# Local attention layers: one slot for both key tiles of half a batch's heads, with the previous slot's weighting behind it; the first sublayer's steps in two parts

## The chip, the cores and the metric

The kernel runs on one core of a Trainium2 chip. Its time is the time of one execution on the device, in microseconds (us); it was run three times. A profile comes from one further execution, whose time is given beside its span (first instruction to last). The engines are named PE (TensorE, matrix products and transposes; PEld is its loading of stationary operands), DVE (VectorE), ACT (ScalarE), POOL (GpSimd) and SP (SyncE, which issues DMAs). Each takes its instructions in the order in which they were issued to it. PE writes to PSUM, which is handed out in banks of 128 partitions x 512 f32.

## The reference: what is computed

The whole program is a chain of sublayers on x, 16 batches of 256 tokens with 128 channels. Two kinds of sublayer bear on the change: the first one of the chain, and the local attention layers, which are run as two pairs (after the first sublayer, and again after a performer sublayer), so four in all.

```python
def _L0_attn_a_ref(x, ...):                     # the first sublayer
    h = _layernorm(x, ln_g, ln_b)
    Q, K, V = h @ Wq.T, h @ Wk.T, h @ Wv.T
    y0 = K @ W0 + (K @ A_init) @ B_init
    gradient = K * (y0 - V)
    grad_shift = cumsum of gradient over the tokens before this one
    correction = Q * lr * grad_shift
    out = y0 - correction * pos_scale
    out = (out * sigmoid(x @ Wg.T)) @ Wo.T * ls_g
    return x + out

def _layer(x, ...):                             # one local layer
    h = shift_token(x)                          # half the channels come from the token before
    q, k, v = split(h @ wqkv, 3)                # 8 heads of 64 each
    q, k = l2norm(q) * qs, l2norm(k) * ksc
    q, k = rotary_xpos(q, k)                    # cos/sin tables over the position
    o = local_attention(q, k, v)                # blocks of 64 queries see their own and the previous block:
    #   mask = (i < j) | (i > j + 64); attn = softmax(where(mask, -max, 8 q k^T)); o = attn v
    x = x + o @ wo
    h = layernorm(shift_token(x)) * lg + lb
    a, g = split(h @ w1 + b1, 2)
    return x + (a * gelu(g)) @ w2 + b2
```

`_L0_attn_a_ref` normalises x with eps 1e-5; in the kernel a norm is made twice over for it, once more for the gate's input. All data are f32; only the mask's product runs in bf16.

## The kernel before

**Helpers.** `mm` (L504) and `tr` (L508) are PE's matmul and transpose; a matmul written out stands at L3465. `act` (L528) is an ACT instruction, `tt` (L531) and `stt` (L543) are DVE's, `gt` (L534) POOL's. All of a helper's instructions carry its line, so they are told apart by their tiles' names. `bank(tag)` (L510) hands out the next PSUM bank of a tag; the banks of a tag go round in order, and a bank is handed out again once everything that reads its last contents is done. `share` (L514) sets how many of the eight banks each tag has in a stage. Inside `manual_schedule` the order in which the program issues its instructions is the order on every engine.

**Tiling.** x and its companions lie with the channels on the partitions: 4096 tokens in 8 chunks of 512 (`NCH`, `CH`), or 32 tiles of 128 (`NTILE`). A batch of 256 tokens is two tiles.

**The first sublayer** (`l0_attn_a`, L1860 to L1947) is a pipeline of steps over the chunks, driven by `slots` (L1820): in slot k step i works on chunk k-i, and within a slot the steps run from the last to the first, and then the steps in `last`. The steps: `enter` (transposes of x), `centre` (`centre_step`, L1759: a product with a centring matrix, a copy by ACT, and a square `nsq` by POOL), `spread` (`spread_step`, L1774: a product with the mean matrix, then Ln and Exp by ACT, twice each), `scale` (two DVE products, and between them ACT's Identity, which adds the bias to `hb`), `gradient` (products for `k` and the error, ACT's copy of `k`, DVE's product and running sum, POOL's scaling by position), `correct` (products for the query, y and the gate; two DVE steps, ACT's Sigmoid, POOL's product with the gate), `out` (a product, DVE, POOL). `last` holds three steps of the next layer's norm, for its first five chunks (`lead`, L1834). ACT's Sigmoid and the Ln/Exp pair need different tables, so the table is loaded anew twice in a slot (`logs`, L1659).

**A local layer** (`local_layer`, L3340) is `local_attend` (L3347 to L3536) and then `local_ffn`, which the change leaves alone. The attention works tile by tile of 128 tokens:

- `project(n)` (L3372): the queries and keys of tile n, two products of 512 columns into two `w` banks; ACT squares both (`sq`), DVE multiplies both by the cosine and the sine table (`t1`, `t2`, four instructions).
- `rotate(n)` (L3390): DVE sums the squares to `ss` (16 values a token) and bounds them; POOL adds the rotated halves into `t1`.
- `unit(n)` (L3400): ACT's Ln and Exp turn `ss` into one over the norm, POOL scales `t1`.
- `turn(n)` (L3408): queries, then keys: four transposes into a `w` bank, which ACT copies to `qkt`; then the values, one product into a `w` bank, which ACT copies to `v`.
- `score(b, hg, t)` (L3423): batch b, half hg of the heads (four), key tile t. Two `s` banks. For t = 0 the four products have 192 columns (128 queries of the tile and 64 of the next), and DVE masks them by a minimum into `pt`, then ACT takes the exponent of both at once (768 columns). For t = 1 the products have 128 columns, and the mask is first put into each bank by a bf16 product of 256 columns; ACT takes the exponent straight from the bank, 256 columns a time. The products of two heads run on the two halves of the array's rows (64 x 128).
- `weigh(b, hg, t)` (L3452): the sums of the weights (a product with ones, bank `pd`) and the weighted values (bank `po`, two halves of 32 of the 64 channels), each as four products that take 32 of the array's columns (128 x 32). After t = 1 ACT takes Ln and Exp(-) of `pd`, into `rd`.
- `divide(b, hg)` (L3478): DVE multiplies `po` by `rd` into `ot`.
- `out(c)` (L3488): chunk c's output product from four slices of `ot`, added to z by DVE.
- `chunk_steps` (L3501): the steps of the norm of x for a chunk (`norm_x_step`, L1811; skipped for the chunks that the stage before has already led), the shift by one token (`shift`, L692, three POOL instructions), and the norm of the result for the feed-forward part (centre, spread, scale with ACT's Identity).

The loop (L3516 to L3536) runs over half-slots k, one for each (b, hg, t), so 64 in all and two for each token tile. In a half-slot the order is: `divide` (of half-slot k-4), `unit`, `score(k)`, `weigh(k-2)`, `project`, `rotate`, `turn`, `out`, `chunk_steps`. A tile is projected ten half-slots ahead of the scores that need it, turned five ahead. The banks: three of `w` (projections, transposes, values, outputs, norms), two of `s`, three of `o`.

Order of the bank requests of `w` in a tile's two half-slots: project twice, queries, keys, values.

Of the kernel before, what the change touches and what calls it, by code (L numbers as in the profile page):

```python
# [13 lines left out]
AF = mybir.ActivationFunctionType  # L14
ALU = mybir.AluOpType
# [1634 lines left out]
class Fast(Net):  # L1650
# [169 lines left out]
    def slots(self, n, *steps, last=(), every=1):  # L1820


        both = (*steps, *last)
        with self.tc.manual_schedule():
            self.logs()
            for k in range((n - 1) * every + len(both)):
                for i in (*reversed(range(len(steps))), *reversed(range(len(steps), len(both)))):
                    c, rest = divmod(k - i, every)
                    if rest == 0 and 0 <= c < n:
                        both[i](c)  # L1830
# [29 lines left out]
    def l0_attn_a(self, w):  # L1860
        nc = self.nc
        with self.second(), ExitStack() as st:
# [26 lines left out]
            sq, rs, cums, ys = {}, {}, {}, {}  # L1889
# [8 lines left out]
            def scale(c):  # L1898
# [3 lines left out]
                self.act(h, h, AF.Identity, bias=w["ln_b"])  # L1902
                self.tt(h0, h0, r1, ALU.mult)

            def gradient(c):
# [8 lines left out]
                self.act(k, pk, AF.Copy)  # L1914
                grad = p.tile([P, CH], F32, tag="grad", name="grad")
# [6 lines left out]

            def correct(c):
                wy, we, lr = made
                h0, h = self.ha[:, self.chunk(c)], self.hb[:, self.chunk(c)]
                pq, py, pg = self.bank(), self.bank(), self.bank()
                self.mm(pq, w["Wq"], h)
                self.mm(py, wy, h)
                self.mm(pg, w["Wg"], h0)
# [4 lines left out]
                g = p.tile([P, CH], F32, tag="g", name="g")  # L1934
                self.act(g, pg, AF.Sigmoid)
# [11 lines left out]
            self.slots(NCH, *first, centre, spread, scale, gradient, correct, out, last=self.lead(p, tables=True))  # L1947
# [1399 lines left out]
    def local_attend(self, w, z, hs, last):  # L3347
# [3 lines left out]

        nc = self.nc
        with ExitStack() as st:
# [16 lines left out]
            made, rot, qkt, val, weights, sums, outs, steps = {}, {}, {}, {}, {}, {}, {}, {}  # L3370
# [37 lines left out]
            def turn(n):  # L3408
                b, t = divmod(n, 2)
                if t == 0:  # L3410
                    qkt[b] = p.tile([P, 2, 4, T], F32, tag="qkt", name="qkt", bufs=2)
                t1, _ = rot.pop(n)
                for i in range(2):
                    pt = self.bank("w")
                    for g in range(4):
                        self.tr(pt[:, g * P : g * P + P], t1[:, i, 2 * g : 2 * g + 2])
                    self.act(qkt[b][:, i, :, t * P : t * P + P], pt.rearrange("p (g t) -> p g t", g=4), AF.Copy)
                pv = self.bank("w")
                self.mm(pv, hs[:, n * P : n * P + P], w["qkv"][:, 1024:])
                val[n] = p.tile([P, 512], F32, tag="v", name="v", bufs=6)  # L3420
                self.act(val[n], pv, AF.Copy)

            def score(b, hg, t):  # L3423
                wide = 192 - 64 * t
                qt, kt = qkt[b][:, 0], qkt[b][:, 1]
                ps = [self.bank("s"), self.bank("s")]
                pt = p.tile([P, 2, 384], F32, tag="pt", name="pt", bufs=4)
                if t:
                    for a in range(2):
                        self.mm(ps[a][:, :T], identb, self.twice(masked), stop=False)  # L3430
                for i in range(2):
                    g = 2 * hg + i
                    for a in range(2):
                        rows = slice(64 * a, 64 * a + 64)
                        self.mm(
                            ps[a][:, i * wide : i * wide + wide], kt[rows, g, t * P : t * P + P],
                            qt[rows, g, t * P : t * P + wide], start=t == 0, stop=t == 0 or i == 1,
                        )
                if t:
                    for a in range(2):  # L3440
                        self.act(pt[:, a, :T], ps[a][:, :T], AF.Exp)
                else:
                    for a in range(2):
                        self.tt(
                            pt[:, a].rearrange("p (i t) -> p i t", i=2), ps[a][:, :384].rearrange("p (i t) -> p i t", i=2),
                            self.twice(w["see"]), ALU.min,
                        )
                    flat = pt.rearrange("p a t -> p (a t)")
                    self.act(flat, flat, AF.Exp)
                weights[b, hg, t] = pt  # L3450

            def weigh(b, hg, t):  # L3452


                wide = 192 - 64 * t
                if t == 0:
                    sums[b, hg] = self.bank("o"), self.bank("o")
                pt = weights.pop((b, hg, t))
                pd, po = sums[b, hg]
                for half in range(-1, 2):  # L3460
                    for r in range(4):
                        i, a = divmod(r, 2)
                        d = (4 * hg + r) * 64 + 32 * half
                        at = max(half, 0) * T + t * P
# [330 lines left out]
```

## Time and profile before

| what | us |
|---|---|
| three runs | 4425.52, 4427.38, 4429.76 (median 4427.38) |
| the profiled execution | 4426.24 |
| its span, first instruction to last | 4424.4 |
| first sublayer, about 14 to 120 | 106 |
| four local attentions, 120-434, 503-799, 1182-1492, 1561-1857 | 314, 296, 310, 296 |
| PE busy in these four | 292, 281, 290, 281 |
| the two feed-forward parts behind the first and the third, 434-503, 1492-1561 | 69, 69 |

The profile is of one execution. Its busy times count, for each engine, the time in which an instruction of it was under way; PE's ends are modelled, so a matmul's start says more than its end. The granted clock is the share of full speed that PE was given; its mean over the span was 0.951. In tables by window the columns are: start and end, length, busy time of PE, PEld, DVE, ACT and POOL with the number of instructions in brackets, granted PE clock, DMA share, GB/s. In a timeline: start, busy time, engine, line, operation, out<-in, shapes, number of like instructions in a row, and in square brackets the idle time before it with what ended it.

In the second local attention (503 to 799) the largest waits were: DVE's multiplies for ACT's squares, 46.9 us in 32 cases; POOL's scaling for ACT's `ss`, 44.2 in 19; ACT's exponents for DVE's minima, 36.9 in 32. PE's own idle time before its groups is a few us in each: before the projections 2.8, before the scores 4.2, before the transposes 4.9.

### The profile page before, as it was taken

The numbers are of one execution on the slowest core, as the hardware profiler recorded it, in microseconds if no ns is written. First come the engines' busy times: TensorE is split into PE (matmuls) and PEld (weight loads), VectorE is DVE, ScalarE is ACT, GpSimd is POOL, SyncE is SP. The second block draws the span as 40 slices with busy tenths as digits, with TensorE's granted clock in tenths as the row PEclk, the third lists the DMA queues.
The fourth block names the chain that finished last, engine by engine and source line by source line (L and its number), as shares of the span: only waits on it lengthen the run. The fifth ranks groups of instructions, "written<-read, shape, count | busy, mean of one in ns | idle before, by whom it ended". The sixth has DMA issues, their size and how long they took to land. (4 is left out here: it accounts for less than half of the span.)

```text
span 4424.4 us, 70817 instructions
## 1 busy us (share of the span) xinstructions
PE 3989.1 (90%) x27720; PEld 2183.8 (49%) x27720; DVE 2620.2 (59%) x4477; ACT 2368.0 (54%) x4505; POOL 2129.9 (48%) x1790
## 2 busy tenths in 40 slices
PE   7899999999899999994989969897999999899978
PEld 3455455466355445553865548653333334355333
DVE  4765576364376376455336633464888788486474
ACT  6665466444766456553337633345565554675442
POOL 4653355232465165315433424465988788521251
PEclk8999999999999999997999979998999999999989
DMA  1800000000000000001630026200000000000000
GB/s 58 331 1 1 10 1 2 19 1 1 19 2 1 1 4 1 1 1 59 204 100 10 15 81 190 70 16 18 1 1 1 2 2 1 15 2 18 6 0 20
DMA packets 70390, 142.31 MB, mean 32 GB/s; under 512 B 11006, under 2 KB 39300, under 8 KB 69920
## 3 DMA queue, kind: packets, MB, share of 16 engines
q1 hardware_dynamic: 57120, 114.46, 7.9%
q0 software_dynamic: 9568, 18.51, 1.2%
q8 instruction: 222, 3.64, 0.3%
q10 hardware_dynamic: 3360, 4.72, 0.3%
q14 instruction: 120, 0.98, 0.1%
HBM read 84.22 MB, written 55.25 MB: 32 GB/s over the span
## 5 line engine op out<-in xcount | busy, mean ns | idle before, releaser
L528 ACT ACTIVATE pt<-ps 128x512 f32<-128x512 f32 (+1 forms) x896 | 423.1, 537 | 410.2 <-PE ps L504 408.8
L504 PE MATMUL ps<-hb,w 128*128 128x512 f32 (+1 forms) x960 | 467.8, 621 | 5.7 <-issue 3.3
L531 DVE TENSOR_TENSOR t<-ps,tab 128x512 f32<-128x512 f32 x512 | 319.6, 684 | 195.5 <-ACT sq L528 190.8
L504 PE MATMUL ps<-w,hb 128*128 128x512 f32 (+2 forms) x896 | 414.9, 576 | 13.8 <-DVE t L531 11.5
L534 POOL TENSOR_TENSOR t<-t,ss 128x1024 f32<-128x1024 f32 x128 | 243.5, 1902 | 309.1 <-ACT ss L528 199.9
L534 POOL TENSOR_TENSOR t<-t,t 128x512 f32<-128x512 f32 x256 | 320.3, 1273 | 13.2 <-PE ps L504 10.1
L504 PEld LDWEIGHTS ps<-hb,w 128*128 128x128 f32 (+1 forms) x960 | 181.9, 194 | 270.3 <-issue 242.2
L504 PE MATMUL ps<-nsq,ct 128*128 128x512 f32 x368 | 212.3, 662 | 70.4 <-POOL nsq L534 51.5
L534 POOL TENSOR_TENSOR nsq<-ha 128x512 f32<-128x512 f32 x112 | 122.5, 1094 | 315.3 <-ACT ha L528 298.7
L531 DVE TENSOR_TENSOR u<-u,ps 128x512 f32<-128x512 f32 x220 | 129.3, 591 | 216.4 <-PE ps L504 144.6
L528 ACT ACTIVATE pt<-pt 128x768 f32<-128x768 f32 (+1 forms) x160 | 169.6, 1060 | 155.4 <-DVE pt L531 155.4
L2185 POOL DMA_INDIRECT back<-y,x x156 | 152.7, 979 | 197.8 <-ACT y L528 171.9
L504 PE MATMUL ps<-qkt 64*128 64x192 f32 (+1 forms) x2048 | 216.9, 327 | 11.8 <-ACT pt L528 11.8
L504 PE MATMUL ps<-u,w 128*128 128x512 f32 (+1 forms) x448 | 218.2, 611 | 8.4 <-POOL u L534 8.4
L504 PE MATMUL ps<-ot,w 128*128 128x512 f32 x448 | 212.2, 607 | 14.8 <-POOL ot L534 6.6
L504 PE MATMUL ps<-xt,w 128*128 128x256 f32 x936 | 219.9, 385 | 4.1 <-DMA w<-in_moe_x 3.1
L504 PEld LDWEIGHTS ps<-qkt 64*128 64x128 f32 x2048 | 153.6, 189 | 134.6 <-ACT qkt L528 51.5
L531 DVE TENSOR_TENSOR pt<-ps,w 128x384 f32<-128x384 f32 (+1 forms) x320 | 171.3, 576 | 77.3 <-PE ps L504 73.9
L504 PEld LDWEIGHTS ps<-w,hb 128*128 128x128 f32 x896 | 147.1, 192 | 139.6 <-issue 110.6
L3692 POOL DMA_INDIRECT rows<-out,idx x128 | 126.3, 987 | 171.4 <-ACT out L528 121.7
L528 ACT ACTIVATE u<-ps,w 128x512 f32<-128x512 f32 x160 | 107.1, 685 | 186.4 <-PE ps L504 183.7
L531 DVE TENSOR_TENSOR pt<-pt,w 128x1024 f32<-128x1024 f32 (+1 forms) x96 | 181.1, 1887 | 42.6 <-ACT pt L528 42.6
(362 smaller groups left out, 9087.5 us busy)
## 6 DMA issues: line engine op xcount, KB each, us to landing
w<-in_moe_x SPq DMA_DIRECT2D x78, 533.0 KB
rows<-t SPq DMA_DIRECT2D x64, 520.0 KB
x<-rows SPq DMA_DIRECT2D x78, 130.0 KB
w<-in_local_f SPq DMA_DIRECT2D x8, 659.5 KB
y<-back SPq DMA_DIRECT2D x16, 256.0 KB
y<-back ACTq DMA_DIRECT2D x16, 256.0 KB
w<-in_local_f SPq DMA_DIRECT2D x4, 658.5 KB
back<-y,x POOLq DMA_INDIRECT x156
```

What stands on the lines that cost most here:

```text
L504: self.nc.tensor.matmul(out, lhsT, rhs, start=start, stop=stop)
L528: self.nc.scalar.activation(out, in_, func, **kw)
L531: self.nc.vector.tensor_tensor(out, a, b, op)
L534: self.nc.gpsimd.tensor_tensor(out, a, b, op)
L2185: nc.gpsimd.indirect_dma_start(views[2 * i + t], bass.IndirectOffsetOnAxis(ap=x[:, t, C : C + 1].bitcast(I32), axis=0), y[:, t], None, bou ...
L3692: nc.gpsimd.indirect_dma_start(views[(c * 2 + k) * 4 + t], bass.IndirectOffsetOnAxis(ap=idx[:, k, t : t + 1], axis=0), out[:, k, t], None,)
```

## The change

**In the first sublayer** a step may be a tuple of two parts. In a slot `slots` first runs part 0 of every step, from the last step to the first, then part 1 of every step that has one in the same order, then the steps in `last`. `scale` keeps its two DVE products as part 0, and the Identity becomes part 1 (`shift`). `gradient` is split behind ACT's copy of `k`: `keys` (products and copy) and the rest. `correct` is split behind the gate: `queries` (the gate's product now first, then query and y, and the Sigmoid) and the rest. No instruction is added or removed.

**In local attention** a slot m is a half of a batch's heads with both key tiles, so 32 slots, one for each token tile. `score(m)` takes four `s` banks: the mask is put into a 128-column piece of each by four bf16 products, then the eight products run one after the other, those of key tile 0 and the first ones of key tile 1 into banks 0 and 1, and the last pair into banks 2 and 3. DVE's minima for tile 0 are as before; ACT's exponents of tile 1 are four of 128 columns, into a tile `pu`, ahead of the wide one. `weigh(m-1)` comes directly behind it, with both key tiles: weighted values first, the sums last. The sums lie in the upper half of the fourth `s` bank of the scores just issued (`spare`), the weighted values in the one `o` bank. Ln and Exp of the sums become a step `inverse`. `turn` makes the values' product and copy first, then both transposes; their copies become a step `keep`.

The order in a slot is now `score(m)`, `weigh(m-1)`, `rotate(m+4)`, `turn(m+2)`, `inverse(m-1)`, `keep(m+2)`, `unit(m+4)`, `divide(m-1)`, `chunk_steps` (with `out`), `project(m+5)`. The banks: three of `w`, four of `s`, one of `o`. Order of the requests of `w` in a slot: values, queries, keys, whatever `chunk_steps` needs, project twice.

```diff
     def slots(self, n, *steps, last=(), every=1):
-        both = (*steps, *last)
+        both = [s if isinstance(s, tuple) else (s,) for s in (*steps, *last)]
...
-                for i in (*reversed(range(len(steps))), *reversed(range(len(steps), len(both)))):
-                    c, rest = divmod(k - i, every)
-                    if rest == 0 and 0 <= c < n:
-                        both[i](c)
+                for some, part in ((range(len(steps)), 0), (range(len(steps)), 1), (range(len(steps), len(both)), 0)):
+                    for i in reversed(some):
+                        c, rest = divmod(k - i, every)
+                        if rest == 0 and 0 <= c < n and part < len(both[i]):
+                            both[i][part](c)
...
                 self.stt(h, h0, w["ln_g"], r2, ALU.mult, ALU.mult)
+                self.tt(h0, h0, r1, ALU.mult)
+
+            def shift(c):
+                h = self.hb[:, self.chunk(c)]
                 self.act(h, h, AF.Identity, bias=w["ln_b"])
-                self.tt(h0, h0, r1, ALU.mult)
...
+            def queries(c):
...
+                pg, pq, py = self.bank(), self.bank(), self.bank()
+                self.mm(pg, w["Wg"], h0)
+                self.mm(pq, w["Wq"], h)
+                self.mm(py, wy, h)
+                g = p.tile([P, CH], F32, tag="g", name="g")
+                self.act(g, pg, AF.Sigmoid)
+                qys[c] = pq, py, g
...
-            self.slots(NCH, *first, centre, spread, scale, gradient, correct, out, last=self.lead(p, tables=True))
+            self.slots(
+                NCH, *first, centre, spread, (scale, shift), (keys, gradient), (queries, correct), out,
+                last=self.lead(p, tables=True),
+            )
...
             def turn(n):
                 b, t = divmod(n, 2)
+                pv = self.bank("w")
+                self.mm(pv, hs[:, n * P : n * P + P], w["qkv"][:, 1024:])
+                val[n] = p.tile([P, 512], F32, tag="v", name="v", bufs=6)
+                self.act(val[n], pv, AF.Copy)
...
+                turned[n] = []
                 for i in range(2):
                     pt = self.bank("w")
                     for g in range(4):
                         self.tr(pt[:, g * P : g * P + P], t1[:, i, 2 * g : 2 * g + 2])
+                    turned[n].append(pt)
+
+            def keep(n):
+                b, t = divmod(n, 2)
+                for i, pt in enumerate(turned.pop(n)):
                     self.act(qkt[b][:, i, :, t * P : t * P + P], pt.rearrange("p (g t) -> p g t", g=4), AF.Copy)
...
+            def score(m):
...
+                ps = [self.bank("s") for _ in range(4)]
+                for x in (*(b[:, 384:] for b in ps[:2]), *(b[:, :P] for b in ps[2:])):
+                    self.mm(x, identb, masked, stop=False)
...
+                for i, t, bank, at in ((0, 0, 0, 0), (1, 0, 0, 192), (0, 1, 0, 384), (1, 1, 2, 0)):
                     for a in range(2):
+                        product(a, i, t, ps[bank + a][:, at : at + 192 - 64 * t])
+                pt = p.tile([P, 2, 384], F32, tag="pt", name="pt", bufs=2)
+                pu = p.tile([P, 4, P], F32, tag="pu", name="pu", bufs=2)
...
+                for i, (bank, at) in enumerate(((2, 0), (0, 384))):
                     for a in range(2):
+                        self.act(pu[:, 2 - 2 * i + a], ps[bank + a][:, at : at + P], AF.Exp)
+                flat = pt.rearrange("p a t -> p (a t)")
+                self.act(flat, flat, AF.Exp)
+                weights[m] = pt, pu
+                spare[0] = ps[3]
+
+            def weigh(m):
+                b, hg = divmod(m, 2)
+                pd, po = spare[0][:, T:] if m < NTILE - 1 else self.bank("s")[:, T:], self.bank("o")
+                pt, pu = weights.pop(m)
+                for half in (0, 1, -1):
+                    for t in range(2):
...
+            def inverse(m):
+                pd, po = sums[m]
+                rd = p.tile([P, T], F32, tag="rd", name="rd", bufs=2)
+                self.act(rd, pd, AF.Ln)
+                self.act(rd, rd, AF.Exp, scale=-1.0)
+                sums[m] = po, rd
...
-            with self.share(w=3, s=2, o=3), self.tc.manual_schedule():
+            with self.share(w=3, s=4, o=1), self.tc.manual_schedule():
...
+                for m in range(-9, NTILE + 9):
+                    if within(m, NTILE):
+                        score(m)
+                    if within(m - 1, NTILE):
+                        weigh(m - 1)
+                    if within(m + 4, NTILE):
+                        rotate(m + 4)
+                    if within(m + 2, NTILE):
+                        turn(m + 2)
+                    if within(m - 1, NTILE):
+                        inverse(m - 1)
+                    if within(m + 2, NTILE):
+                        keep(m + 2)
+                    if within(m + 4, NTILE):
+                        unit(m + 4)
+                    if within(m - 1, NTILE):
+                        divide(m - 1)
+                    chunk_steps(m)
+                    if within(m + 5, NTILE):
+                        project(m + 5)
```

`chunk_steps` counts in slots of four to a chunk: `out` and the second `shift` of chunk c in slot 4c+5, the norm of the result in 4c+6, 4c+7 and 4c+8, the first `shift` in 4c-6, the norm of x in 4c-9 to 4c-7.

## The prediction

> **What bounds the kernel now.** I read the page first, then the busy time of each stage that the change touches (the first sublayer, and the first two of the four local attentions), then the order of one cycle on each engine.
>
> ```profile
> PE 3989.1 (90%) x27720; PEld 2183.8 (49%) x27720; DVE 2620.2 (59%) x4477; ACT 2368.0 (54%) x4505; POOL 2129.9 (48%) x1790
> ```
>
> ```profile
> 14.00:120.00 106.00, 79.57 (x174) 33.47 (x173) 54.38 (x68) 73.74 (x105) 46.99 (x48) 0.89 0.08 30
> 120.00:434.00 314.00, 292.33 (x2665) 163.15 (x2664) 205.43 (x312) 191.05 (x422) 172.74 (x157) 0.98 0.30 115
> 503.00:799.00 296.00, 280.97 (x2652) 159.96 (x2651) 198.47 (x305) 184.49 (x412) 165.98 (x148) 0.99 0.02 5
> ```
>
> Local attention is TensorE's: 281 of 296 us, VectorE 67%, ScalarE 62%. The four take 1216 us of the 4424 us span, the first sublayer about 106. One cycle of TensorE there (two half-slots, one token tile):
>
> ```profile
> 641.24 0.38 PE L504 MATMUL ps<-masked,identb 128*128 128x256 bf16 x2
> 641.55 0.71 PE L504 MATMUL ps<-qkt 64*128 64x128 f32 x8
> 642.19 0.43 PE L3465 MATMUL ps<-pt,ct 128*32 128x128 f32 x8
> 642.43 0.62 PE L3465 MATMUL ps<-pt,v 128*32 128x128 f32 x16
> 642.99 1.09 PE L508 MATMUL ps<-ct,t 128*128 128x128 f32 x8
> 643.91 1.02 PE L504 MATMUL ps<-w,hb 128*128 128x512 f32 x2
> 644.87 0.92 PE L504 MATMUL ps<-qkt 64*128 64x192 f32 x8
> 645.72 0.53 PE L3465 MATMUL ps<-pt,ct 128*32 128x192 f32 x8
> 646.07 0.83 PE L3465 MATMUL ps<-pt,v 128*32 128x192 f32 x16
> 646.83 1.98 PE L504 MATMUL ps<-w,hb 128*128 128x512 f32 x4
> ```
>
> Starts count here, since the ends are modelled. Start to start the groups take 0.31, 0.64, 0.24, 0.55, 0.92, 0.96, 0.85, 0.35, 0.76 and 1.82: 7.40 us. In a long run a 512-column record steps by 0.43 us (eight output records in 3.43), so 128 columns are 0.107 and 192 are 0.161. Four weight strips or two row halves share one step. By that the cycle would be 6.32; the other 1.08 us lie where the array's shape changes (64*128, 128*32, 128*128), six times a cycle: 0.21 into and through each score group, 0.15 each weighting, 0.1 elsewhere. With the extras of four cycles (four output matmuls, two of the norm) and one stall of 1.18 the first squares lie 10.85, 8.28, 8.28, 8.60 apart: 36.01 us a group. Where a chunk's first norm is still to be made (three chunks in the first and third stages), groups take 41.04, one 39.47.
>
> The other engines' rows give the steps of the new chain:
>
> ```profile
> 646.88 0.84 ACT L528 ACTIVATE pt<-pt 128x768 f32<-128x768 f32 x1 [1.30 <-DVE pt L531]
> 648.00 0.60 ACT L528 ACTIVATE sq<-ps 128x512 f32<-128x512 f32 x1 [0.28 <-PE ps L504]
> ```
>
> ```profile
> 645.82 1.02 DVE L531 TENSOR_TENSOR pt<-ps,w 128x384 f32<-128x384 f32 x2 [1.41 <-PE ps L504]
> 648.62 2.49 DVE L531 TENSOR_TENSOR t<-ps,tab 128x512 f32<-128x512 f32 x4 [1.78 <-ACT sq L528]
> ```
>
> ```profile
> 659.24 0.45 ACT L528 ACTIVATE ss<-ss 128x16 f32<-128x16 f32 x2
> 659.60 0.64 ACT L528 ACTIVATE pt<-ps 128x256 f32<-128x256 f32 x2
> 660.13 0.39 ACT L528 ACTIVATE rd<-ps 128x256 f32<-128x256 f32 x1
> 660.54 0.42 ACT L528 ACTIVATE rd<-rd 128x256 f32<-128x256 f32 x1
> 660.87 1.07 ACT L528 ACTIVATE qkt<-ps 128x512 f32<-128x512 f32 x2
> ```
>
> ```profile
> 505.20 2.29 PE L504 MATMUL ps<-w,hb 128*128 128x512 f32 x4 [0.46 <-DVE t L531]
> ```
>
> The multiplies of a projection start only after ScalarE's square of the same bank (0.62 after its start), though both only read: I take one bank as one engine's at a time. The last line is the second projection's second matmul waiting for the multiplies of the first one's first bank: the three `w` banks go round in order, and a freed bank restarts TensorE 0.15 us later, with 0.08 more for the first matmul.
>
> **What the change does to TensorE's own time.** Score, weighting and shape changes are once a slot instead of twice: shapes change three times. Masks become four of 128 columns, which no row shows: between 0.21 (half the 0.107 of a 256-column one) and 0.43 (each as long as 128 columns of f32); I take 0.32. Then 0.10 gap, score 4x0.107+4x0.161+0.21=1.28, weighting 6x(0.107+0.161)+0.15=1.76, values 0.96, transposes 0.86, projection 1.72: 7.00, or 0.4 less than before. The Trainium skill, "TensorE: Matmul & The Clock Gate", Back-to-back issue gap, gives about 81 ns a matmul at 128 columns among weight loads; by it the masks are an estimated 0.32.
>
> **What it puts on the path.** In a slot the banks of tag `w` are taken in the order values, two transposes, extra, two projections. So an extra takes the bank of the values, the first projection (or, without extra, the second) that of the first transposes, and it waits for ScalarE's `keep` copy. That stands in ScalarE's queue behind the four small exponents, the wide one, the `v` copy, Ln and Exp; and the wide exponent waits for VectorE's two minima, now queued behind the four multiplies of the projection before. From one first square to the next this is: 0.62 to the multiplies, 2.41 for them, 1.06 for the minima, one small exponent (128 columns, no row: between the 0.12 step of 16 columns and 0.27 of 256; I take 0.17), wide exponent 0.76, `v` 0.50, Ln 0.41, Exp 0.33, two copies 0.95, the two `ss` 0.36: 7.57. The values are first visible 4.62 into a slot (4.42 plus the 0.20 from TensorE to ScalarE), the `v` copy starts there or 5.02 after the square, and the first `keep` copy ends 1.83 later.
>
> With x the first square's start in its slot's frame, by slot mod 4: slot 2 (norm centre, x=-0.66): copy ends 6.45, projection 6.60 to 8.40. Slot 3 (norm spread): the same, 8.40; ScalarE's Ln and Exp (1.25) bring x to 0.02. Slot 0: `v` at 5.04, second projection from 7.02, 7.96; the norm's Identity brings x to 0.43. Slot 1: `v` at 5.45, so the output matmuls wait until 6.20, 11.43. Group: 36.19 against 36.01. **The 0.4 us a slot is given back to the banks.** The added wait of the sums (ones) for the exponent of the fourth score bank costs nothing: it ends near 2.24 in slot 1, the sums start at 2.82; 0.58 later it would hold up all of TensorE. The second tile's four exponents (0.17 each) lie in ScalarE's wait for the minima; without that wait they cost 0.14 a slot over two of 256. Division and the single `ot` buffer wait for the output matmuls in slot 1 (to 9.9, then 0.69) and end before the multiplies at 11.4. POOL's adds, scaling and shifts (5.6 of 9 us) end a slot ahead of their transposes. No DMA moves.
>
> Groups with a first norm I make 38.4 (0.8 in slot 3, 0.5 in slot 0, 0.9 in slot 2, where VectorE's `ha` multiply delays the projection's): 41.04 had a 2.4 us wait for POOL's square, which now has a slot more. Per stage 5.5 groups: first stage 2.5x0.18-3x2.6=-7.4, third 2.5x0.18-1.1-2x2.6=-5.9, second and fourth +1.0 each. The four early slots without extras take 7.57 for 7.42: +2.4 in all. The five last slots without projection are TensorE's, 0.4 less each: -8. Together -17.
>
> **First sublayer.**
>
> ```profile
> 54.98 0.72 ACT L528 ACTIVATE hb<-hb,w 128x512 f32<-128x512 f32 x1 [3.15 <-DVE hb L543]
> ```
>
> ```profile
> 49.50 1.04 POOL L534 TENSOR_TENSOR nsq<-ha 128x512 f32<-128x512 f32 x1 [3.81 <-ACT ha L528]
> ```
>
> The Identity's wait (about 3.1, six times) goes, as it is emitted last. But POOL's square now stands ahead of its y multiply: y, five matmuls to k (4.46), 0.20, k 0.61, table 1.29, two Ln 1.17, two Exp 1.04, copy 0.62, square 1.00, y 1.27: 11.7 a slot against 10.1 to 10.9 for three slots (+3.5). The start loses 3, the three slots with the next norm some 4. TensorE then idles 4.1 us a slot, and the one like idle here (4.4 us to 99.1) was followed by 3.4 us at granted clock 0.5: 1.7 each, two or three times. Sum 0, bounds -19 (waits alone) and +10 (three slots and four half clocks). Nothing is late but the hand-over, which follows.
>
> **Sum**: -17. The profiled execution took 4426.2 (span 4424.4 and 1.8 around it), the runs' median 4427.4: 4410.
>
> **A rule against the change.** The Trainium skill, "TensorEngine Tiling (Array Packing)", PSUM Bottleneck, says that packing speeds TensorE but not the copies out of PSUM, and asks to take several tiles of a bank in one access; here two exponents of 256 become four of 128. By the busy rows alone TensorE stays the bound and the time is 4335; by the rule the copies bound it, as the chain above says on its own.
>
> **Rivals.** (B) Slower: the chain is longer than its rows. Place: the projection's wait for `keep`, price 12.8 us for each 0.1 us a slot (128 slots). From 0.13 us it eats the gain; at 0.4 the time is 4411+51=4462. For it: eight in-order steps, each with a possible wait unseen. Against: all have rows. (C) The bank waits hide (the chain is shorter, or the copy earlier): TensorE alone, 4x7.00+3.43+1.72=33.2 a group, -2.8x5.5-2-1.6=-19 a stage, -15 more from five norm groups: 4335. For it: today it is the bound; against: the bank order seen at 505.20. (D) It does not do what it says: shape changes remain as many; then 0.4 more a slot, a case of B.
>
> **Chances.** The bound for no change is 0.2%, 8.9 us. Forecast 0.58 (own range 4385 to 4436, 0.2 us a slot; masks and small exponent are 7 and 5 of it): faster 0.38, same 0.16, slower 0.04. B 0.30, nearly all slower; C 0.12. Faster 0.50, same 0.17, slower 0.33. Range 4365 to 4465: it leaves out C and the far end of B.
>
> **What would show it.** Right: groups near 36.2 us; projection matmuls with idle time released by ACT qkt; output matmuls by ACT v; ScalarE waiting some 2 to 3 us for DVE pt; three shape changes in 7.0 us of work. Wrong: TensorE without idle (C); idle over 1 us a slot, or granted clock under 0.95 in the stage at 503 (B); Identity waits gone and a first sublayer shorter by over 10 us.

## The result, and the profile after

| kernel | median of its runs, us | ratio to before, 95% interval |
|---|---|---|
| before (the three runs above and two more) | 4426.7 | |
| changed | 4406.4 (4402.4 to 4408.5) | 0.9951 [0.9940, 0.9963] |

The forecast was 4410. The profiled execution of the changed kernel took 4408.54 (span 4406.7), 17.7 less than that of before. The page's first part, then the first sublayer and the second local attention in the columns shown before:

```profile
PE 3972.6 (90%) x27976; PEld 2218.2 (50%) x27976; DVE 2594.5 (59%) x4477; ACT 2376.2 (54%) x4761; POOL 2139.3 (49%) x1790
```

```profile
14.00:120.00 106.00, 82.97 (x174) 35.70 (x173) 54.30 (x69) 74.10 (x105) 47.97 (x49) 0.84 0.08 31
492.00:783.00 291.00, 276.19 (x2714) 168.17 (x2712) 193.27 (x303) 187.11 (x476) 166.00 (x145) 0.99 0.02 5
```

By busy shares nothing moved: TensorE has 276 of 291 us in the attention, 95% as before, and the first sublayer runs at a lower granted clock, 0.84. Where the time went is read off two of ScalarE's rows in each layer: the first square of its attention (`sq`) and the last Gelu of its feed-forward part (`u`). The first layer's, before and then after:

```profile
120.62 0.60 ACT L528 ACTIVATE sq<-ps 128x512 f32<-128x512 f32 x1
496.19 0.68 ACT L528 ACTIVATE u<-ps,w 85x512 f32<-85x512 f32 x1 [1.03 <-PE ps L504]
```

```profile
120.79 0.60 ACT L528 ACTIVATE sq<-ps 128x512 f32<-128x512 f32 x1 [2.71 <-PE ps L504]
484.87 0.68 ACT L528 ACTIVATE u<-ps,w 85x512 f32<-85x512 f32 x1 [1.03 <-PE ps L504]
```

First square at 120.6 before, 120.8 after, so the first sublayer gave nothing in this pair of profiles. From there to the last Gelu the four layers took 375.6, 366.8, 371.7 and 366.8 before and 364.1, 366.8, 363.3 and 366.6 after: 11.5, 0.0, 8.5 and 0.2 less, 20.2 in all. Four slots make a group: slot 1 holds the output products, slots 2 and 3 products of the result's norm. A plain group, measured from one tile's first square to that of the tile four later, went from 36.00 to 35.73. Groups of the first and third layer in which a chunk's first norm is made as well ("norm groups" below) went from 41.05 to 37.47.

TensorE's timeline over slots 0 and 1 of a group of the changed kernel (second layer; start, busy time, and in brackets the idle time with what ended it):

```profile
652.65 1.04 PE L508 MATMUL ps<-ct,t 128*128 128x128 f32 x8
654.03 2.33 PE L504 MATMUL ps<-w,hb 128*128 128x512 f32 x4 [0.34 <-ACT v L528]
656.20 0.39 PE L504 MATMUL ps<-masked,identb 128*128 128x128 bf16 x4
656.51 1.37 PE L3459 MATMUL ps<-qkt 64*128 64x192 f32 x16
...
659.58 1.13 PE L504 MATMUL ps<-w,hb 128*128 128x512 f32 x2
660.54 1.04 PE L508 MATMUL ps<-ct,t 128*128 128x128 f32 x8
662.35 3.70 PE L504 MATMUL ps<-ot,w 128*128 128x512 f32 x8 [0.77 <-ACT v L528]
665.89 1.88 PE L504 MATMUL ps<-w,hb 128*128 128x512 f32 x4
667.60 0.39 PE L504 MATMUL ps<-masked,identb 128*128 128x128 bf16 x4
```

The transposes take 1.38 and 1.81 to the next start where 0.87 is their own (it is 0.87 in a run below without the wait): TensorE waits twice, for the bank that the `v` copy frees. The projection of slot 0 takes 2.17 to the next start, and 1.80 in that run: there TensorE waits a third time, for the bank that `keep` frees. ScalarE's timeline of slot 1 says why:

```profile
656.12 0.72 ACT L528 ACTIVATE hb<-hb,w 128x512 f32<-128x512 f32 x1
656.74 1.07 ACT L528 ACTIVATE sq<-ps 128x512 f32<-128x512 f32 x2
660.33 0.28 ACT L528 ACTIVATE pu<-ps 128x128 f32<-128x128 f32 x1 [1.98 <-DVE pt L531]
660.80 0.28 ACT L528 ACTIVATE pu<-ps 128x128 f32<-128x128 f32 x1 [0.19 <-DVE pt L531]
660.97 0.84 ACT L528 ACTIVATE pt<-pt 128x768 f32<-128x768 f32 x1
661.71 0.59 ACT L528 ACTIVATE v<-ps 128x512 f32<-128x512 f32 x1
662.92 1.07 ACT L528 ACTIVATE qkt<-ps 128x512 f32<-128x512 f32 x2
```

The values' product ended by 660.71 (659.58 and 1.13); the `v` copy starts at 661.71, directly behind the wide exponent, which stands behind VectorE's minima (1.98 idle). The first line is the result norm's Identity, with no wait. In the kernel before it had one. ScalarE and TensorE there, in a plain group:

```profile
704.35 0.72 ACT L528 ACTIVATE hb<-hb,w 128x512 f32<-128x512 f32 x1 [2.35 <-DVE hb L543]
```

```profile
705.75 1.19 PE L504 MATMUL ps<-qkt 64*128 64x192 f32 x8 [0.84 <-ACT pt L528]
```

and in a group with a first norm:

```profile
294.40 0.72 ACT L528 ACTIVATE hb<-hb,w 128x512 f32<-128x512 f32 x1 [2.35 <-DVE hb L543]
```

```profile
297.38 1.55 PE L504 MATMUL ps<-nsq,ct 128*128 128x512 f32 x2 [2.42 <-ACT qkt L528]
```

ScalarE waited 2.35 us for VectorE's multiply by `hb`, which stood behind the projection's four multiplies, and everything behind the Identity was late with it: an exponent that frees an `s` bank, and the copy of the queries that frees a `w` bank (the first of two `qkt` copies ended at 297.23; the norm's product took its bank at 297.38). These 2.42 us are the wait that the prediction put down to POOL's square, which had long ended:

```profile
289.05 1.06 POOL L534 TENSOR_TENSOR nsq<-ha 128x512 f32<-128x512 f32 x1
```

Whether ScalarE's wait carried the gain was for the experiments.

### The profile page after: what moved, and what is told of

Read it like the earlier page. It is cut to its first block, busy times and chain, and to the rows that moved or that the text cites. A ratio compares the mean times of both kernels' runs of the same rounds, so it can differ in the third digit from the quotient of the medians.

```text
span 4406.7 us, 71429 instructions
## 1 busy us (share of the span) xinstructions
PE 3972.6 (90%) x27976; PEld 2218.2 (50%) x27976; DVE 2594.5 (59%) x4477; ACT 2376.2 (54%) x4761; POOL 2139.3 (49%) x1790
## 5 line engine op out<-in xcount | busy, mean ns | idle before, releaser
L528 ACT ACTIVATE pt<-ps 128x512 f32<-128x512 f32 x640 | 339.8, 600 | 311.0 <-PE ps L504 309.6
L504 PE MATMUL ps<-w,hb 128*128 128x512 f32 (+2 forms) x896 | 436.6, 595 | 31.7 <-DVE t L531 12.3
L531 DVE TENSOR_TENSOR ot<-ps,rd 128x512 f32<-128x512 f32 (+1 forms) x208 | 136.5, 656 | 240.6 <-ACT rd L528 127.5
L528 ACT ACTIVATE pu<-ps 128x128 f32<-128x128 f32 x512 | 125.7, 276 | 256.6 <-DVE pt L531 158.7
L528 ACT ACTIVATE nrs<-ps,ct 128x512 f32<-128x512 f32 x208 | 139.7, 684 | 107.9 <-PE ps L504 102.6
L528 ACT ACTIVATE sq<-ps 128x512 f32<-128x512 f32 x256 | 144.0, 589 | 93.1 <-PE ps L504 93.1
```

The costliest lines, as they stand in the source:

```text
L504: self.nc.tensor.matmul(out, lhsT, rhs, start=start, stop=stop)
L528: self.nc.scalar.activation(out, in_, func, **kw)
L531: self.nc.vector.tensor_tensor(out, a, b, op)
```

## The experiments

All were timed against the kernel before on the same chip. "First square" is where the first sublayer ends, "layers" is the sum of the four stretches from first square to last Gelu, and the groups are read from the tiles' first squares, plain ones in the second layer, norm groups in the first and third. Times are medians; the last four columns are from one profile of each.

| run | time | ratio, interval | first square | layers | plain group | norm group |
|---|---|---|---|---|---|---|
| before | medians of 4426.7 to 4429.4 | | 120.6 | 1481.0 | 36.00 | 41.05 |
| changed | 4406.4 | 0.9951 [0.9940, 0.9963] | 120.8 | 1460.8 | 35.73 | 37.47 |
| local alone | 4404.9 | 0.9945 [0.9931, 0.9958] | 121.1 | 1459.8 | 35.73 | 37.47 |
| first alone | 4419.2 | 0.9980 [0.9971, 0.9989] | 118.5 | 1480.6 | 36.00 | 41.05 |
| keep first | 4445.0 | 1.0037 [1.0023, 1.0051] | 117.2 | 1503.5 | 38.05 | 38.69 |
| early square | 4431.2 | 1.0005 [0.9996, 1.0015] | 122.2 | 1482.2 | 36.00 | 41.35 |
| square late | 4390.1 | 0.9915 [0.9901, 0.9928] | 105.7 | 1463.7 | 35.74 | 37.48 |
| minima between | 4362.7 | 0.9855 [0.9840, 0.9870] | 116.5 | 1423.7 | 34.25 | 36.03 |
| keep first, scaled | 4395.8 | 0.9928 [0.9915, 0.9942] | 114.3 | 1453.8 | 35.32 | 37.19 |
| Identity late | 4385.6 | 0.9904 [0.9889, 0.9919] | 120.6 | 1436.4 | 34.82 | 36.81 |
| all four | 4343.8 | 0.9811 [0.9797, 0.9824] | 107.4 | 1408.6 | 33.88 | 35.34 |
| minima and square | 4352.0 | 0.9830 [0.9816, 0.9843] | 105.8 | 1422.4 | 34.25 | 36.03 |
| scale behind | 4427.6 | 0.9997 [0.9988, 1.0006] | 118.8 | 1487.6 | 36.70 | 38.6 to 40.2 |
| before plus | 4369.7 | 0.9869 [0.9854, 0.9884] | 104.2 | 1437.6 | 34.82 | 36.81 |

### Which part of the change?

Local attention as changed, the first sublayer as before (the old step list, no parts):

> The change in local attention alone, with the first sublayer as before. Theory (the time comes from local attention: 11.5, 0, 8.5 and 0.2 us in the four layers by the two profiles, and the first sublayer gives nothing): about 4406 us, as the whole change. Rival (the first sublayer gave part of it, and its slower middle slots hide that): 4412 us or more.

It took 4404.9, the whole change's time. And the reverse:

> The change in the first sublayer alone, local attention as before. Theory (two effects that cancel: three middle slots some 4 us longer, the last ones some 3 us shorter each): no change, within 4 us of the 4427 of before, and the first square of local attention within 1 us of 120.6. Rival (Identity's waits of about 3.1 us, six times, were on the path): 4415 us or less.

4419.2, 9.5 less than its runs of before: neither the theory's 4427 nor the rival's 4415. The first square came 2.1 us earlier and the layers are the same (1480.6 and 1481.0); the rest of the 9.5 lies in the rest of the program, which no run here changes. By the profiles (span less first square and layers) that rest took 2822.8 us before, 2825.1 in the changed kernel, 2820.4 in local alone and 2819.0 in first alone, and 2819.0 to 2829.2 over all fourteen. Why it differs is not shown; a few us between two times say nothing on the part that was changed unless its own stretch shows them. It is also why local attention alone was no slower than the whole change: its first square is within 0.4 us and its layers within 1.1 us of the changed kernel's. Over all profiles the first sublayer ends at 114.3 to 120.8 in its changed form (six runs without the late square, mean 117.7) and at 120.6 to 122.2 in the old one (four, mean 121.1). The two effects are there: the time from one slot's output product to the next was 10.4, 12.7, 9.3 in the middle and 14.4, 12.5, 9.0, 7.5 at the end before; it is 14.8, 14.3, 13.5 and then 9.5, 8.4, 7.0, 6.9. They cancel but for 1.6 us in this pair of profiles, and some 3 over all.

### Is it POOL's square?

In the kernel before, the first norm's centring a half-slot earlier:

```diff
-                    for i, slot in enumerate((-17, -15, -13)):
+                    for i, slot in enumerate((-18, -15, -13)):
```

> The kernel before with the centring step of the norm of x half a slot pair earlier (from the end of an odd half-slot to the end of the even one before it), so that POOL's square lies ahead of the scaling and the adds. Theory (the groups of 41.05 us had TensorE wait 2.4 us for that square, and the change gained by giving it a whole slot): 38 to 39 us a group, five of them, 11 to 13 us less than before: about 4415. Rival (those groups are longer for the products and copies of the norm themselves): 4427, and no group under 40.5.

No: 41.35, and the time is that of before. Then the Identity, one half-slot later and so behind the copies, still in the kernel before (the multiply stays where it was):

```diff
                 for i, slot in enumerate((12, 14, 16)):
...
-                        steps[1][i]()
...
+                            self.stt(s, s, w["lg"], steps[1], ALU.mult, ALU.mult)
+                if (c := at(k, 17, 8, NCH)) is not None:
+                    s = hs[:, self.chunk(c)]
+                    self.act(s, s, AF.Identity, bias=w["lb"])
```

> The kernel before with the result norm's Identity on ScalarE one half-slot later, behind the copies of the transposes. Theory (the groups of 41.05 us had TensorE wait 2.42 us for a w bank that ScalarE's copy of the keys frees, and that copy stood behind the Identity's own wait of 2.35 us for VectorE): these groups fall to 38 to 39 us, the others stay at 36.0; 11 to 13 us less than before, about 4416. Rival (POOL's square after all): no group changes, 4428.

In a plain group the Identity now starts without a wait and the scores follow the values' product at once, and in a norm group the norm's product does so too:

```profile
685.23 0.71 ACT L528 ACTIVATE hb<-hb,w 128x512 f32<-128x512 f32 x1
```

```profile
683.67 1.02 PE L504 MATMUL ps<-w,hb 128*128 128x512 f32 x2
684.63 0.92 PE L504 MATMUL ps<-qkt 64*128 64x192 f32 x8
```

```profile
288.54 1.02 PE L504 MATMUL ps<-w,hb 128*128 128x512 f32 x2
289.40 1.02 PE L504 MATMUL ps<-nsq,ct 128*128 128x512 f32 x2
```

The mechanism was right (but for the copy: it is that of the queries) and its reach too small: it takes 4.24 off a norm group and also 1.18 off every plain one, 44.6 in the layers. One instruction moved in the old kernel, without merged slots, beats the whole change by 21 us. The wait of ScalarE is 2.35 in both kinds of group: a plain one had hidden half of it, a norm group paid more than the wait itself.

So the change is two things of opposite sign. Taking that wait away is worth 44.6 in the layers of the old kernel (1481.0 to 1436.4). Merged slots instead of half-slots then cost 24.4 (1436.4 to 1460.8), though TensorE's own work is shorter.

### The waits of the merged slot

`keep` ahead of `inverse` on ScalarE:

```diff
-                    if within(m - 1, NTILE):
-                        inverse(m - 1)
                     if within(m + 2, NTILE):
                         keep(m + 2)
+                    if within(m - 1, NTILE):
+                        inverse(m - 1)
```

> The changed kernel with keep (ScalarE's two copies of the transposes) issued ahead of inverse (Ln and Exp of the sums), so that the copies come 0.81 us earlier. Theory (TensorE's projection waits for the banks that keep frees): slot 0 loses its wait of 0.78 us, the slots with norm products some 0.3 each, and the output's wait for the v copy (0.86) stays; 1.1 to 1.5 us a group of four slots, the early slots of 7.51 go towards 7.1: 4370 to 4382 us. Rival C (TensorE's own work sets the time): no change, 4406. A second rival (rd then comes late and the one bank of the weighted values is freed late): 4400 or more.

The opposite: 4445.0, a slot of 8.32 had become 10.86. From mask to mask the slots with norm products did win 0.28 and 0.22, about as expected; but slot 0 won only 0.06 of its 0.78, and the early slots stayed at 7.51. VectorE's and POOL's rows at the end of slot 0, and ScalarE's:

```profile
666.61 2.30 DVE L543 SCALAR_TENSOR_TENSOR hb<-hb,w,nrs 128x512 f32<-128x512 f32 x1
```

```profile
666.47 1.90 POOL L534 TENSOR_TENSOR t<-t,ss 128x1024 f32<-128x1024 f32 x1 [2.02 <-ACT ss L528]
```

```profile
668.95 0.72 ACT L528 ACTIVATE hb<-hb,w 128x512 f32<-128x512 f32 x1 [2.62 <-DVE hb L543]
```

The multiply by `hb`, 0.74 us in the changed kernel and the one before, takes 2.30: POOL's scaling began 0.14 us before it and ran to 668.37, and the multiply ended 0.54 after that. `inverse` later means division later, and so the multiply fell into POOL's scaling; the Identity came late, the exponents behind it too, and the sums held up TensorE for 2.16 us. The cure keeps the order and moves only the multiply:

```diff
                         rotate(m + 4)
+                    scaled(m)
...
+            def scaled(m):
...
+                    self.stt(s, s, w["lg"], steps[1], ALU.mult, ALU.mult)
```

> keep ahead of inverse as in the run before, and the norm's multiply by hb on VectorE moved from behind the division to behind rotate, where no POOL instruction of two operands runs. Theory (that run lost 2.2 us a group only because this multiply, 0.74 us alone, took 2.30 beside POOL's scaling, and won 0.28 in each of two slots): the multiply takes 0.74, groups are 35.0 to 35.3 us, the time 4388 to 4397 us. Rival (keep first is slower for itself): groups of 38 again, 4445 us.

```profile
646.35 0.74 DVE L543 SCALAR_TENSOR_TENSOR hb<-hb,w,nrs 128x512 f32<-128x512 f32 x1
```

0.74 again, groups of 35.32, 4395.8. Next, the chain ahead of the exponents: VectorE's minima between the projection's multiplies.

```diff
                         score(m)
+                    if within(m + 4, NTILE):
+                        multiply(m + 4, 1)
...
             def project(n):
-                for i in range(2):
-                    for m, t in enumerate((t1, t2)):
...
+                multiply(n, 0)
```

> The changed kernel with VectorE's two minima of a slot ahead of the last two of the four multiplies of the projection before, so that the exponents come 1.2 us earlier. Theory (the wait for ScalarE's copies, behind the exponents, sets slots 0 and 1): the output's wait for the v copy (0.86) goes, slot 0 loses about 0.5, slots 2 and 3 keep their 0.3; groups of 35.73 become 34.3 to 34.5, the time about 4375 us. Rival C (TensorE's own work): 4406. Second rival (the later multiplies hold up the rotation on POOL or the projection's second bank): 4400 or more.

4362.7, with groups of 34.25: the groups as the theory had them, the total 12 us better. The layers fell by 37.1, some 33 of it in 22 groups of -1.48 and the rest mostly in the early slots; the first square came 4.3 earlier than in the changed kernel's profile and the rest of the program took 6.0 less, neither of which this edit touches. ScalarE now waits for TensorE ahead of the values, and not for VectorE ahead of the exponents:

```profile
659.57 0.84 ACT L528 ACTIVATE pt<-pt 128x768 f32<-128x768 f32 x1
661.39 0.60 ACT L528 ACTIVATE v<-ps 128x512 f32<-128x512 f32 x1 [0.98 <-PE ps L504]
```

That rules out rival C: with TensorE's work unchanged the layers fell by 37 us.

The third step of the result's norm put back behind the projection, in the changed kernel:

```diff
                         project(m + 5)
+                    scaled(m)
...
+            def scaled(m):
...
+                    self.stt(s, s, w["lg"], steps[1], ALU.mult, ALU.mult)
+                    self.act(s, s, AF.Identity, bias=w["lb"])
```

> The changed kernel with the third step of the result's norm (VectorE's multiply and ScalarE's Identity) put where the kernel before had it: behind the projection. Theory (what the change gained in the groups is that this step no longer stands behind the projection's four multiplies; the merged slot alone loses): the Identity waits some 3 us after the squares, the exponents of the fourth score bank come behind it, about 5.4 us into the slot, and the sums, due at 2.8, hold up TensorE; 2 to 2.6 us a group, groups of 37.7 to 38.4, the time 4440 to 4460, slower than before. Rival (ScalarE waits for the minima there anyway, so the Identity fits into that wait): at most 0.7 us a group, 4406 to 4422.

ScalarE and TensorE in slot 1:

```profile
667.71 0.72 ACT L528 ACTIVATE hb<-hb,w 128x512 f32<-128x512 f32 x1 [2.72 <-DVE hb L543]
```

```profile
668.82 0.53 PE L3495 MATMUL ps<-pt,ct 128*32 128x192 f32 x8 [1.72 <-ACT pu L528]
```

The chain is the theory's, link by link: Identity 2.72 late, the sums 1.72 behind it. But a group costs only 0.97 more, not 2 to 2.6, as the output's wait for the `v` copy in the same slot (0.9) is gone in exchange; norm groups cost 1.2 to 2.8 more. With 4427.6 the whole gain of the change is gone: 0.9997 [0.9988, 1.0006]. The place of this one step decides whether the change is worth anything. The two things do not simply add: with the wait in both kernels merging costs 6.6 in the layers (1481.0 to 1487.6), without it 24.4.

### First sublayer: the square behind y

```diff
-                NCH, *first, centre, spread, (scale, shift), (keys, gradient), (queries, correct), out,
+                NCH, *first, (centre, square), spread, (scale, shift), (keys, gradient), (queries, correct), out,
```

> The changed kernel with POOL's square of the first sublayer's centring step in part 1, so behind the product with the gate and the scaling by position, and ahead of nothing that TensorE needs in that slot. Theory (in the changed first sublayer three slots take 14.2 us on average because y waits behind the square, TensorE idles 4.1 to 4.7 us and then runs at half clock): these slots fall to 8 to 10 us, the first square of local attention comes 10 to 16 us earlier than 120.8, the time is 4390 to 4397 us. Rival (ScalarE's table loads and norms set the slot): 4402 us or more.

TensorE and POOL in the changed kernel, then POOL with the square late:

```profile
42.87 2.08 PE L504 MATMUL ps<-y,w 128*128 128x512 f32 x2 [4.70 <-POOL grad L1925]
```

```profile
40.55 1.04 POOL L534 TENSOR_TENSOR nsq<-ha 128x512 f32<-128x512 f32 x1 [3.49 <-ACT ha L528]
41.55 1.26 POOL L534 TENSOR_TENSOR y<-y,g 128x512 f32<-128x512 f32 x1
```

```profile
38.66 1.27 POOL L534 TENSOR_TENSOR y<-y,g 128x512 f32<-128x512 f32 x1 [6.27 <-DVE y L531]
...
42.53 1.49 POOL L534 TENSOR_TENSOR nsq<-ha 128x512 f32<-128x512 f32 x1
```

y stood behind a square that waited for ScalarE; TensorE idled 4.70 us. With the square late the three slots take 9.1, 11.0 and 10.4, the first square of local attention comes 15.1 us earlier, and the time is 4390.1, at the theory's near end.

### All together

> The changed kernel with two of these edits, the square late and minima between. Theory: the two are in different stages and add up, 16 and 44 us off 4406: 4346 to 4352 us, groups of 34.25 as with the minima alone.

> The changed kernel with four edits together: the square late (first sublayer), minima between the multiplies, keep ahead of inverse, and the norm's multiply behind rotate. Theory (each removes a wait of its own: 14 to 16 us at the start, 1.5 us a group for the minima, 0.3 in each of slots 2 and 3 and up to 0.3 in slot 0 for keep): groups of 33.3 to 33.6 us, TensorE's own work, and a time of 4325 to 4345 us. Rival (the waits for the copies and for the minima are one and the same, so that keep first brings nothing more): groups of 34.2, 4345 to 4352.

> The kernel before with two small edits and without the merged slots: the result norm's Identity one half-slot later, and the changed first sublayer with its square late. Theory (43 us and some 14 us, in different stages): 4368 to 4374 us, groups of 34.8 and 36.8. It shows what is to be had without merging; merged slots with all their waits removed should be 1.3 us a group shorter.

The stages add up (4352.0, 4369.7; the last is the kernel before with the Identity late and the first sublayer of the run with the square late). All four edits give 4343.8, 1.9% under before and the best version found; its groups of 33.88 lie 0.3 above the theory's end, with a wait of 0.39 ahead of the second transposes for VectorE's last multiply, now the later one:

```profile
626.60 0.66 PE L508 MATMUL ps<-ct,t 128*128 128x128 f32 x4 [0.39 <-DVE t L531]
```

With the waits away, merged slots do win: 33.88 against 34.82, and 26 us in the time. The old slots had only one edit of attention against three, but little is left in them: by the prediction's steps their own work is 4x7.40+3.43+1.72 = 34.75 a plain group. That is what merging can give, and the change as it stands did not collect it.

## Why the prediction was right, and where it was not

- **TensorE's own time**: right. 7.00 predicted; slots without extras take 7.01 and 7.02 in the run with all four edits. The masks take 0.32 as assumed and as estimated, scores 1.29, weighting 1.78, values 0.96, transposes 0.87, projection 1.72 to 1.80.
- **The chain of 7.57**: right. The early slots of the changed kernel lie 7.51 apart; moving the minima, one of its links, brought them to 7.36, and `keep` as well to 7.01, TensorE's own time. `keep` alone left them at 7.51: it changes the order on ScalarE and not the length of the chain.
- **Slots**: 8.40, 8.40, 7.96, 11.43 predicted; 8.22, 8.22, 7.89, 11.40 from mask to mask. The `keep` copy's end in the norm slots was put 0.2 too late, so the group became 35.73 and not 36.19.
- **"It is given back to the banks"**: right, and shown by both runs that moved copies or exponents. But the reference for it was wrong: 36.00 held a stall of 1.18 that the prediction listed and did not explain. Without it the old slot is 34.82, so the merged one gives back more than it saves, 0.9 a group. That the copies out of PSUM, and not TensorE, would bound the time is what the rule set against the change said.
- **Groups with a first norm**: the step that failed is its cause, "a 2.4 us wait for POOL's square, which now has a slot more". The square had ended at 290.1, seven us ahead of the product; the bank was late, as the queries' copy stood behind the Identity. The size, 38.4 for 37.47, was near by luck: the change moved the true cause as well.
- **Early slots**: +0.6 a layer predicted. The second layer shows it: five groups bring -1.4, the end -2 by the same kind of rows, the sum is 0, so the start costs about +3.4. The groups' error and this one cancel there.
- **First sublayer**: 0 predicted, about -3 found over all profiles. Both halves were there and each too small: three slots +10.1 instead of +3.5 and two or three half clocks of 1.7; the later slots -11.7 instead of about -4. The half clock was under-sized: it lasted 6.8 us, twice 3.4, around and behind the idle times of the first two slots, as below. The idle time that it was sized by, "4.4 us to 99.1", is 4.25 in TensorE's row.
- **"0.58 later it would hold up all of TensorE"**: shown, by 1.72 us when the Identity was put in front of that exponent.

By layer the prediction adds up to -8.8, -0.4, -7.3 and -0.4; measured were -11.5, 0.0, -8.5 and -0.2, and the rest of the program, put at nothing, took 2.3 more in this pair of profiles. The total came out 3.6 us from the forecast with two causes wrong in it, so part of its closeness is luck. Of the 9.5 us that the first sublayer showed alone, some 6 lie outside of it, and why is open.

## What to carry to other kernels

Before costing what a change adds, explain every stall of the kernel before: a stall of 1.18 us in a group of 36, and of 4.24 in one of 41, was worth more than the rewrite around it, and it lay in one instruction that waits in an in-order queue ahead of copies which free banks. When steps are merged, ask what each bank's last reader stands behind; work that TensorE no longer does is worth nothing until that chain is as short as the new slot.

## What the runs showed of the hardware

**VectorE beside POOL.** In these traces a VectorE instruction that reads two tensors from SBUF waits for a POOL product that is under way. With `keep` first, the multiply by `hb` took 2.30 us in the ten groups of the first two layers where POOL's scaling had begun before it, ending 0.54 or 0.55 after POOL's end, and 0.74 or 0.75 in the other 38 cases in those layers of this run, the changed kernel and the one before. It was not free of POOL in every later run: it took 1.37 in 19 cases of the run with the Identity late and 1.81 or 1.82 in 18 of the one with all four edits, again ending 0.55 after a POOL product. The bound on `ss` (16 columns) in the kernel before took 0.17 in the 20 cases without a POOL product under way and 0.83 in the median of the 108 with one, ending 0.03 after POOL. The reverse shows in POOL's late square: 1.49 instead of 1.04, where it began 0.59 before the end of such a VectorE multiply. The minima and the multiplies of the projection, with one input in PSUM, run at their usual 0.55 and 0.68 beside POOL.

The Trainium skill, "SBUF — State Buffer", Who interferes with whom, says that a VectorE instruction with two SBUF inputs contends with a GpSimd one that reads SBUF, that the ports they share are an exclusive lock, and that the order of issue decides which one waits. These rows agree, in both orders.

**Half clock around idle times.** Stretches of the first sublayer by window, one slot each, before and after (the last columns are granted clock, DMA share and GB/s):

```profile
42.60:53.00 10.40, 7.82 (x20) 3.36 (x20) 6.81 (x8) 7.16 (x10) 5.26 (x7) 1.00 0.00 0
```

```profile
42.80:57.60 14.80, 10.64 (x20) 4.59 (x20) 6.41 (x7) 6.36 (x10) 5.32 (x7) 0.73 0.00 0
```

The same 20 matmuls take 10.6 instead of 7.8 us. TensorE idled 2.5 us at most around them in the one case and 4.7 just ahead of them in the other: 0.73 over 14.8 us is a clock halved for some 8 us of the slot. Where it was halved, in the changed kernel:

```profile
42.20:49.10 6.90, 6.23 (x8) 2.62 (x9) 4.91 (x5) 0.78 (x2) 3.62 (x4) 0.51 0.00 0
55.90:62.70 6.80, 5.08 (x6) 2.19 (x7) 4.16 (x4) 1.64 (x2) 4.68 (x5) 0.50 0.00 1
73.00:76.40 3.40, 3.40 (x6) 1.32 (x5) 3.37 (x4) 1.66 (x2) 3.18 (x3) 0.50 0.00 0
```

The idle times there were 4.70 (to 42.87), 4.12 (to 57.62) and 3.32 (to 71.89). The prediction had taken one such stretch of 3.4 us from the idle time before 99.1. The length of an idle time alone does not say what follows: in the kernel before, the clock was also 0.51 from 62.3 to 65.8 and from 86.2 to 89.7, behind idle times of 2.50 and 2.02, while another of 2.50, to 50.59, lies in the stretch above at 1.00.
